# Loading x2 for the last layer's sum into a tile of its own, issued one body earlier

## The chip, the cores and the metric

One core of a Trainium2 chip runs the whole kernel. The metric is device time in microseconds (us), lower is better; where several runs were made the median is given.

## What is computed

The reference is a network of two blocks on an image of 4 x 128 channels x 64 x 64. The first block adds an attention layer and then a recurrence over the 4096 positions. The second adds a stack of eight Mamba layers and then a layer of experts. Around the change it is this line:

```python
x = x + _L1_conv_ref(_ln_c(x), L1_conv_W_in, ...)     # eight Mamba layers, then the sum
```

`_ln_c` normalizes over the channels. Each Mamba layer projects its input, applies a short causal convolution, forms `dA = exp(dt * A)` and `dBx = dt * xc * B` for 16 states a channel, runs `h = dA * h + dBx` along the positions, sums `h * C` over the states, gates the result, projects back and normalizes. The x that the sum takes is the recurrence's output, which the kernel calls x2; the sum is x3.

## The kernel before, in words

The data lies with channels on the 128 partitions and positions along the free axis. The function `mamba` works through 256 bodies: 8 chunks of 512 positions, in each chunk 8 layers, in each layer the 4 images (`bodies`, L1167). Body number i is thus of the last layer where i mod 32 is 28 to 31, and of the first layer of a chunk where it is 0 to 3.

A body is walked through in 16 slots (L1227 to 1256). In each slot, VectorE runs two scans (L1075), the next slot's dBx is made on TensorE (L1042), ScalarE makes dA a few slots ahead (L1020), GpSimd multiplies a group of four states by C in every second slot (L1100), and TensorE adds up products of four slots before (L1104). For the two slots in the middle, 8 and 9 counted from 1, GpSimd makes the scan's input instead of TensorE (L1063).

The rest of the work is put into the slots by hand, in the table `PLAN` (L711), one row for a slot. In a row, what stands left of the bar comes before TensorE adds up, what stands right after it. The letter says whose work it is: o the body whose scans run, n the next one, q the one before, s and z the bodies three and four further on if they are of the first layer. All engines run their instructions in program order, and `manual_schedule` keeps the order as written; so the table is also the order of each queue.

The rows that matter here, numbered from 1:

- row 1, `s.mean` (L838 to 841): the mean of x2 for a body of the next chunk, made in the tile that `z.fetch` filled; row 2 takes its variance
- row 11, `| q.u n.diag q.end`: the norm of the body before (L1154, on VectorE), the load of the next body's diagonal blocks (`diag`, L1014, 1792 KB), and `end` of the body before
- row 12, `n.dtx0` (L979): GpSimd multiplies dt by the input for the next body; `n.turn0` in row 15 turns it on TensorE (L986), and only then can the next body's dBx be made
- row 13, `z.fetch` (L834): loads x2 of a first-layer body four further on, 256 KB
- row 14, `n.C0` (L957): the first of four loads of C for the next body, 1024 KB each

`end` does something only for the last layer's bodies, 32 in all. It takes a tile under the tag "x2", of which there is one buffer, the same that `fetch` and `mean` use; loads x2 into it (L1159); adds the layer's output on GpSimd (L1160); and stores the sum to x3 in DRAM (L1163). All DMAs here are issued by SyncE, which stands at an issue until what that issue must wait for is done; only the last store of all is ScalarE's. The recurrence of the first block runs alongside in the first 220 bodies, some steps in each slot (L670 to 700), with loads and stores of its own on the same queue.

Of the kernel before, what the change touches and what calls it, by code (L numbers as in the profile page):

```python
# [8 lines left out]
F32 = mybir.dt.float32  # L9
# [11 lines left out]
P = 128  # L21
# [19 lines left out]
DEPTH = 8  # L41
# [5 lines left out]
TL = 512  # L47
# [673 lines left out]
n.bt q.ru s.first n.spread n.B n.skip0 |  # L721
| q.u n.diag q.end
n.pt0 n.softplus0 n.pt1 n.dtx0 | o.leave0 n.softplus1
o.back0 | z.fetch
| n.C0
n.turn0 |
n.C1 n.dtx1 | n.skip1 o.gate0
# [19 lines left out]
def mamba(tc, ops, I, rec, x2_d, x3_d):  # L747
# [8 lines left out]
    nc = tc.nc  # L756
# [7 lines left out]
    with ExitStack() as ctx:  # L764
# [8 lines left out]
        w1 = ctx.enter_context(tc.tile_pool(name="mw1", bufs=1))  # L773
# [38 lines left out]
        def bank(what):  # L812

            name = f"f{BANK[what]}"
            return psf.tile([P, TL], F32, tag=name, name=name)
# [27 lines left out]
        def sums(o, of, what):  # L843

            o.ms = bank(what)
            for n in range(NB):
                nc.tensor.matmul(  # L847
                    o.ms[:, n : n + 1], of[:, n * P : (n + 1) * P], ops.avg[:, 0:1],
                    start=n == 0, stop=True, skip_group_check=True,
                )  # L850

        def inverse(o, eps):

            o.r = w.tile([P, NB], F32, tag="r", name="r")
            nc.vector.tensor_scalar(o.r, o.ms[:, 0:NB], eps, None, ALU.add)
            nc.gpsimd.tensor_tensor(o.r, o.r, power, ALU.pow)

        def rows(o, what):

            o.R = bank(what)  # L860
            for n in range(NB):
                nc.tensor.transpose(
                    o.R[:, n * P : (n + 1) * P], o.r[:, n : n + 1].to_broadcast([P, P]), ops.ident
                )
# [287 lines left out]
        def norm(o):  # L1152
            o.out = us[o.b] = up.tile([P, TL], F32, tag="u", name="u")
            nc.vector.tensor_tensor(o.out, o.pos, o.R, ALU.mult)  # L1154

        def end(o):
            here = (slice(None), o.b, slice(o.ck * TL, (o.ck + 1) * TL))
            x3 = w1.tile([P, TL], F32, tag="x2", name="x3")
            nc.sync.dma_start(out=x3, in_=x2_d[here])  # L1159
            nc.gpsimd.tensor_tensor(x3, x3, o.out, ALU.add)  # L1160

            by = nc.scalar if o is bodies[-1] else nc.sync
            by.dma_start(out=x3_d[here], in_=x3)  # L1163
# [5 lines left out]
        def get(i):  # L1169
            return bodies[i] if 0 <= i < len(bodies) else None  # L1170

        def table(name):
            return lambda o: nc.scalar.preload_act_table_set(name)
# [16 lines left out]
            "B": give_b,  # L1190
            "bt": turn_b, "square": square, "pm": lambda o: sums(o, o.sq, "pm"),
            "rstd": lambda o: inverse(o, 1e-5), "ru": lambda o: rows(o, "ru"), "u": norm,
            "end": lambda o: end(o) if o.l == DEPTH - 1 else None, "edge": edge, "edges": add_edge,
            "exp": table(EXP_TANH),
        }
# [21 lines left out]
        for i in range(-2, len(bodies) + 1):  # L1217
            o, n, q = get(i), get(i + 1), get(i - 1)
            who = {"o": o, "n": n, "q": q, "m": get(i + 2), "a": o or q}
            s, z = get(i + 3), get(i + 4)  # L1220
# [362 lines left out]
@with_exitstack  # L1583
def tile_kernel(ctx: ExitStack, tc: tile.TileContext, I, out):
    nc = tc.nc
    const = ctx.enter_context(tc.tile_pool(name="const", bufs=1))
    dram = ctx.enter_context(tc.tile_pool(name="scratch", bufs=1, space=DRAM))
    nc.scalar.preload_act_table_set(EXP_LN)
    ops = Ops(nc, const)
    stats = const.tile([P, B * NBLK, 6], F32, name="stats")  # L1590
    gating_w = gating_weights(tc, const, ops, I)
    x1_d = dram.tile([P, B, L], F32, name="x1_d")
    x2_d = dram.tile([P, B, L], F32, name="x2_d")
    x3_d = dram.tile([P, B, L], F32, name="x3_d")
    wx_d = dram.tile([P, B, L], F32, name="wx_d")

    with tc.manual_schedule():
        with ExitStack() as c:
            conv_layer(tc, ops, I, x1_d, wx_d, stats)
            rec = Recurrence(c, tc, ops, I, stats, wx_d, x1_d, x2_d)  # L1600
            mamba(tc, ops, I, rec, x2_d, x3_d)
        experts(tc, ops, I, gating_w, x3_d, out)
# [90 lines left out]
```

## Time and profile before

| | |
|---|---|
| median of 3 runs | 15102.85 us (15088.36 to 15107.24) |
| the profiled execution, its own time | 15096.43 us |
| its span | 15094.6 us |
| TensorE clock granted in it | 0.978 of full |
| scans of `mamba`, first to last start | 1945.2 to 14807.7 us |
| DMA: moved, mean rate | 1914.56 MB, 127 GB/s |
| diag load, x256 | 1792 KB each, 8.8 us median from issue to landing |
| C load, x1024 | 1024 KB each, 6.7 us median |
| x3 store, x31 on SyncE | 256 KB each, 2.0 us median |

The page of a profile lists busy time by engine (PE is TensorE, PEld its weight loads, DVE is VectorE, ACT is ScalarE, POOL is GpSimd, SPq the DMA queue of SyncE) and groups of equal instructions with busy time, mean duration in ns, and the idle time just before them with what ended it. The timeline lists instructions in order of time: start, duration, engine, line, operation, output and inputs, and in brackets the idle time before it. Tile names have their numbers left out, so x stands for x2 and x3 tiles alike, x_d for the DRAM arrays that hold them. A view of one line of code gives its instructions, what its engine waited for ahead of them, and, for a DMA, the time from issue to landing. A wait for several things is put down to the one that ended last in the profile.

### The profile page before, as it was taken

How to read it: one execution, taken by the hardware profiler on the slowest of the kernel's cores; microseconds unless marked ns; L12 is line 12 of the kernel's file. 1: busy time of each engine (PE TensorE's matmuls, PEld its weight loads, DVE VectorE, ACT ScalarE, POOL GpSimd, SP SyncE). 2: the span in 40 equal slices, each digit the busy share in tenths (PEclk: the TensorE clock that was granted, in tenths of full speed). 3: DMA queues.
4: the chain of work that ended last, by engine and by line, in shares of the span. 5: the costliest groups of instructions: out<-in, count | busy, mean ns of one | idle time of the engine just before them, and what ended most of it. 6: DMA issues, size and time to landing. Idle time of an engine off the chain costs nothing. (4 is left out here: it accounts for less than half of the span.)

```text
span 15094.6 us, 307827 instructions
## 1 busy us (share of the span) xinstructions
PE 14211.8 (94%) x124378; PEld 10858.4 (72%) x124378; DVE 12976.4 (86%) x16043; ACT 10979.7 (73%) x21400; POOL 12587.4 (83%) x5760
## 2 busy tenths in 40 slices
PE   7999989999999999999999999999999999999996
PEld 3444577777777777777777777777777777777774
DVE  8996079998999899989998899989998999889984
ACT  6887267776777677777777777777777777677772
POOL 5664079998999899989998899989998999889983
PEclk8999999999999999999999999999999999999998
DMA  0001034343444343334434333433343344334344
GB/s 23 26 26 35 15 133 145 136 145 136 143 141 141 139 148 139 138 136 149 139 139 147 139 142 136 148 136 139 139 148 137 135 144 148 134 130 146 130 144 180
DMA packets 600045, 1914.56 MB, mean 127 GB/s; under 512 B 347489, under 2 KB 347873, under 8 KB 434273
## 3 DMA queue, kind: packets, MB, share of 16 engines
q1 hardware_dynamic: 598480, 1894.60, 35.6%
q8 instruction: 984, 16.12, 0.4%
q14 instruction: 437, 3.57, 0.1%
q10 hardware_dynamic: 144, 0.26, 0.0%
HBM read 1823.10 MB, written 71.57 MB: 126 GB/s over the span
## 5 line engine op out<-in xcount | busy, mean ns | idle before, releaser
L1100 POOL TENSOR_TENSOR hs<-hs,Cb 128x2048 f32<-128x2048 f32 x2048 | 9295.1, 4540 | 718.5 <-DVE state L1092 547.6
L1075 DVE TENSOR_TENSOR_SCAN hs<-dA,state,dBx 128x512 f32<-128x512 f32 x7168 | 8804.6, 1266 | 919.3 <-PE dBx L1042 772.2
L1020 ACT ACTIVATE dA<-dt,A 128x512 f32<-128x512 f32 x7168 | 4730.3, 716 | 16.3 <-DVE hs L1075 10.2
L1104 PE MATMUL yT<-ident,hs 128*128 128x128 f32 x32768 | 4404.3, 278 | 139.1 <-POOL hs L1100 138.9
L1042 PE MATMUL dBx<-diag,dtxT 64*128 64x128 f32 x57344 | 4214.1, 284 | 24.8 <-DVE hs L1075 18.2
L1104 PEld LDWEIGHTS yT<-ident,hs 128*128 128x128 f32 x32768 | 3803.7, 147 | 548.3 <-issue 354.3
L1042 PEld LDWEIGHTS dBx<-diag,dtxT 64*128 64x128 f32 x57344 | 3526.8, 187 | 803.7 <-issue 746.8
L683 PEld LDWEIGHTS p<-z,vt 128*128 128x128 f32 x8192 | 1283.6, 189 | 854.0 <-ACT z L691 374.2
L691 ACT ACTIVATE z<-p 128x4 f32<-128x4 f32 x4096 | 702.4, 171 | 1514.3 <-PE p L683 1486.6
L683 PE MATMUL p<-z,vt 128*128 128x4 f32 x8192 | 1452.2, 248 | 80.5 <-ACT z L691 71.6
L1075 DVE TENSOR_TENSOR_SCAN hs<-dAp,state,hs 128x512 f32<-128x512 f32 x1024 | 1272.4, 1271 | 296.7 <-POOL hs L1063 296.7
L1063 POOL TENSOR_TENSOR hs<-Bb,dtx 128x512 f32<-128x512 f32 x1024 | 1282.8, 1276 | 0.0
L904 DVE SCALAR_TENSOR_TENSOR xc<-f,taps,xc 128x511 f32<-128x511 f32 (+2 forms) x1536 | 1112.2, 724 | 28.1 <-ACT z L691 24.0
L1020 ACT ACTIVATE dAp<-dt,A 128x512 f32<-128x512 f32 x1024 | 708.8, 692 | 490.6 <-DVE hs L1075 455.8
L279 DVE SCALAR_TENSOR_TENSOR acc<-qp,dww,acc 128x512 f32<-128x512 f32 x1184 | 892.0, 753 | 25.6
L979 POOL TENSOR_TENSOR dtx<-dt,xc 128x512 f32<-128x512 f32 x512 | 651.3, 1272 | 217.5 <-ACT dt L973 217.5
L293 POOL TENSOR_TENSOR off<-off,to 128x512 f32<-128x512 f32 x288 | 366.6, 1273 | 411.3 <-ACT to L291 398.6
L1020 ACT ACT_TABLE_LOAD x511 | 655.6, 1283 | 9.0
L898 ACT ACTIVATE xc<-f,taps 128x512 f32<-128x512 f32 x512 | 350.7, 685 | 426.4 <-PE f L895 293.7
L919 PE MATMUL f<-u,given 128*128 128x512 f32 x1024 | 601.5, 671 | 3.9 <-DVE xc L904 3.8
L847 PEld LDWEIGHTS f<-avg,sq 128*128 128x128 f32 x2048 | 257.4, 197 | 466.2 <-ACT sq L1148 466.2
L895 PE MATMUL f<-u,given 128*128 128x512 f32 x1024 | 567.0, 636 | 0.8 <-DVE u L868 0.8
(235 smaller groups left out, 15145.7 us busy)
## 6 DMA issues: line engine op xcount, KB each, us to landing
Cb<-c_d SPq DMA_DIRECT2D x1024, 1024.0 KB, 6.7
diag<-spare SPq DMA_DIRECT2D x256, 1792.0 KB, 8.8
Bb<-c_d SPq DMA_DIRECT2D x256, 512.0 KB, 4.9
given<-in_m_given_dram SPq DMA_DIRECT2D x64, 640.0 KB, 8.2
slab<-in_w_dram SPq DMA_DIRECT2D x60, 512.0 KB, 9.9
x<-x_d SPq DMA_DIRECT2D x96, 256.0 KB, 3.7
c_d<-dbl SPq DMA_DIRECT2D x512, 32.0 KB, 1.6
x_d<-x SPq DMA_DIRECT2D x63, 256.0 KB, 2.0
```

The costliest lines, as they stand in the source:

```text
L279: nc.vector.scalar_tensor_tensor(rows(to), x, dww[:, t : t + 1], rows(o.acc), ALU.mult, ALU.add)
L683: nc.tensor.matmul(self.p[:, k, :], self.vt, self.before, start=False, stop=True, skip_group_check=True)
L691: nc.scalar.activation(self.z[:, k, :], self.p[:, k, :], AF.Tanh, scale=0.5)
L904: nc.vector.scalar_tensor_tensor(x, o.v[h][:, : TL - k], taps[:, o.l, h, DC - 1 - k : DC - k], x, ALU.mult, ALU.add)
L919: nc.tensor.matmul(o.pz[h], o.given[:, at : at + P], o.u, start=True, stop=True)
L979: nc.gpsimd.tensor_tensor(to, blocks(o.dt[h]), blocks(o.xc[:, h, :]), ALU.mult)
L1020: nc.scalar.activation(o.dA[j][:, k, :], o.dt[h], AF.Exp, scale=A[:, o.l, h, n : n + 1])
L1042: nc.tensor.matmul(o.dBx[j][:, at : at + 64, :], o.dtxT[h][row, n, :], o.diag[row, n, :, 2 * sp : 2 * sp + 2], start=True, stop=True,)
L1063: nc.gpsimd.tensor_tensor(hs[:, k, :].rearrange("p (q n t) -> p q n t", n=NB, q=2), o.Bb[:, k, :].rearrange("p (q n t) -> p q n t", n=NB, ...
L1075: nc.vector.tensor_tensor_scan(hs[:, k, :], o.dA[j][:, k, :], hs[:, k, :] if sp == SP_B else o.dBx[j][:, :, k], state[:, o.l, o.b, h, s : ...
L1100: nc.gpsimd.tensor_tensor(hs, hs, o.Cb[f], ALU.mult)
L1104: nc.tensor.matmul(o.yT[:, n, :], x[:, n * P : (n + 1) * P], ops.ident, start=start and n == 0, stop=True, is_transpose=True, skip_group_c ...
```

## The change

The load in `end` becomes a step of its own, `x3`, that fills a tile under a tag of its own ("x3", again one buffer), and the table puts it into row 13 of the body that it belongs to, ahead of `z.fetch`. `end`, still in row 11 of the body after, takes that tile. Lines are otherwise as before, and 2 KB per partition more of the on-chip memory are used.

```diff
-o.back0 | z.fetch
+o.back0 o.x3 | z.fetch
...
+        def fetch_x(o):
+
+            o.x3 = w1.tile([P, TL], F32, tag="x3", name="x3")
+            nc.sync.dma_start(out=o.x3, in_=x2_d[:, o.b, o.ck * TL : (o.ck + 1) * TL])
+
         def end(o):
             here = (slice(None), o.b, slice(o.ck * TL, (o.ck + 1) * TL))
-            x3 = w1.tile([P, TL], F32, tag="x2", name="x3")
-            nc.sync.dma_start(out=x3, in_=x2_d[here])
+            x3 = o.x3
             nc.gpsimd.tensor_tensor(x3, x3, o.out, ALU.add)
...
+            "x3": lambda o: fetch_x(o) if o.l == DEPTH - 1 else None,
```

## The prediction

> **What bounds the kernel now.** I read the page first. VectorE, GpSimd and TensorE are all close to full, so a stall on one can reach the end, and the scan is what the recurrent stage is paced by:
>
> ```profile
> PE 14211.8 (94%) x124378; PEld 10858.4 (72%) x124378; DVE 12976.4 (86%) x16043; ACT 10979.7 (73%) x21400; POOL 12587.4 (83%) x5760
> ...
> L1075 DVE TENSOR_TENSOR_SCAN hs<-dA,state,dBx 128x512 f32<-128x512 f32 x7168 | 8804.6, 1266 | 919.3 <-PE dBx L1042 772.2
> ```
>
> The scan waits 772.2 us in all for its input dBx from TensorE. To see where, I cut the span at the first scan of each body (32 scans a body, 256 bodies, numbered in their order) and asked for the busy time of the engines by stretch. Columns: stretch, length, busy PE, PEld, DVE, ACT, POOL, clock, DMA.
>
> ```profile
> 3319.20:3368.60 49.40, 48.38 (x448) 38.74 (x447) 45.28 (x52) 37.76 (x73) 46.41 (x21) 1.00 0.46 161
> 3368.60:3427.40 58.80, 52.20 (x459) 42.12 (x458) 46.70 (x56) 39.73 (x76) 47.61 (x21) 0.93 0.40 143
> 3427.40:3487.20 59.80, 52.69 (x459) 42.42 (x459) 46.60 (x54) 38.78 (x74) 47.13 (x21) 0.93 0.37 129
> ```
>
> These are bodies 28, 29 and 30. Body 28 takes 49.4 us, much as those before it; the bodies in which the one before was of the last layer (29, 30, 31, 32 and the same places of each later chunk) take 57.8 to 62.1, with only 1.4 us more VectorE and 1.2 us more GpSimd work. Thirty periods are of this kind: four for each of seven chunks, and two in the last chunk.
>
> The timeline of body 29 shows how the stall arises. VectorE:
>
> ```profile
> 3418.76 0.67 DVE L1136 TENSOR_TENSOR y<-f,gate 128x512 f32<-128x512 f32 x1
> 3427.37 1.28 DVE L1075 TENSOR_TENSOR_SCAN hs<-dA,state,dBx 128x512 f32<-128x512 f32 x1 [7.94 <-PE dBx L1042]
> ```
>
> GpSimd, and below it SyncE's queue:
>
> ```profile
> 3403.83 4.54 POOL L1100 TENSOR_TENSOR hs<-hs,Cb 128x2048 f32<-128x2048 f32 x1 [1.14 <-DVE state L1092]
> 3416.23 1.26 POOL L1160 TENSOR_TENSOR x<-x,u 128x512 f32<-128x512 f32 x1 [7.87 <-DMA x<-x_d]
> 3417.45 1.26 POOL L979 TENSOR_TENSOR dtx<-dt,xc 128x512 f32<-128x512 f32 x1
> ```
>
> ```profile
> 3406.12 0.34 SPq L1014 DMA_DIRECT2D diag<-spare  x1
> 3406.57 0.38 SPq L1159 DMA_DIRECT2D x<-x_d  x1
> 3417.52 0.32 SPq L1163 DMA_DIRECT2D x_d<-x  x1
> 3419.53 0.32 SPq L834 DMA_DIRECT2D x<-x_d  x1
> 3419.90 3.64 SPq L957 DMA_DIRECT2D Cb<-c_d  x2
> ```
>
> The load of x3 (L1159) is issued 0.45 us behind the 1792 KB load of diag. GpSimd is done at 3408.37 and waits 7.87 us for it at the sum (L1160); dtx, next on GpSimd, starts at 3417.45 though its dt was ready near 3409.2 (body 28: dtx at 3358.60, 0.92 us after GpSimd was free). dtx must be turned on TensorE before the next body's dBx can be made, and the first scan of that body is 7.94 us late.
>
> Over all 32 sums, the view of line 1160 lists GpSimd's idle time ahead of it:
>
> ```profile
>   DMA x<-x_d: 93.8, 12
>   DVE state L1092: 74.6, 10
>   DVE hs L1075: 51.1, 6
>   issue: 16.0, 2
>   DVE u L1154: 2.1, 1
> ```
>
> That is 237.6 us. Only 93.8 carry the DMA's name, but the other engines named had been done: in each of the 30 cases the sum begins 8.0 to 10.5 us after the load was issued, and u was ready some 11 us before (3405.45 against 3416.23). The view of line 1159 gives the landing times:
>
> ```profile
> DMA to landing us min/median/max: 2.7/9.1/10.4
> ```
>
> Leaving out the 2.1 us of the very last sum (a true wait for u), 235.5 us, or 7.85 for each of 30, is waiting for this load. VectorE's gaps before the 30 first scans that follow run from 6.9 to 9.5 us and sum to 237.9: the stall goes over to the scan nearly one to one.
>
> **The change, part by part.**
>
> *Load out of slot 11.* Removes GpSimd's 7.85 us wait 30 times. In its place the sum starts at 3408.37, ends at 3409.6, and dtx runs 3409.6 to 3410.9 instead of 3417.45: 7.85 us earlier. The sum's own 1.26 us stays on GpSimd, but 0.92 of it lies where dtx waits for dt anyway, so dtx is 0.4 us later than in body 28. That is covered: the scans of the old body keep VectorE busy to 3419.43. Were the cover gone, it would cost 0.4 x 30 = 12 us. The first scan falls back to 3419.43, a gain of 7.9 us.
>
> A rule of the Trainium skill speaks against so much. "DMA: Bandwidth & Descriptors", section "Anatomy of one DMA — SWDGE (gpsimd) path", gives a DMA about 2.0 us plus its bytes at 436 GB/s: 2.6 us for 256 KB (an estimate, for the GpSimd path). The load would then land at 3409.2 and GpSimd wait 0.8 us: 30 x 0.8 = 24 us to gain. The trace has 2.8 us for the same size when nothing is ahead (x2's load of 3419.53), but a median of 9.1 for this one, behind diag. The row decides: 7.85.
>
> *What is late next.* After the stall, body 29 is 58.80 - 7.94 = 50.9 us, against 49.4: its VectorE does 1.4 us more (mean and first norm of the next chunk). GpSimd's 47.6 us and TensorE's 52.2 stand below or near that; of TensorE's, part is the cold restart (clock 0.93 against 1.00), which goes with the stall. Cold restarts cost something between nothing (body 31: 58.4 - 7.5 = 50.9) and 0.8 us (body 30: 59.8 - 8.1 = 51.7) in the 22 periods that begin so: 0 to 18 us. I take 0.2 each, 4 us, nearer to body 31.
>
> *Load into slot 13 of its own body, with its own tile.* The same number of DMAs, the same bytes, 0.38 us of SyncE's time each. It has a whole body (about 50 us) until its sum, so its landing costs nothing even behind diag (10.4 us at most). The tile has one buffer, so in bodies 29, 30 and 31 of a chunk the load waits until the previous body's x3 is stored. Behind it on SyncE stand the x2 fetch, the Cb loads and, every fourth body, the recurrence's loads. Before, the x2 fetch itself waited for that store (L834 after L1163), so the wait isn't new, only its place.
>
> How long it is, the trace doesn't show: the store will be issued at 3409.7, with diag still in flight. On the near side is its row now, 2.0 us with the queue empty: landing at 3411.7. On the far side is the same page, section "Queues, rings and completion order": each DMA engine takes descriptors in ring order, so the store ends behind diag, where the load ended, at 3406.57 + 9.5 = 3416.1. I take the far end. Then x3's load goes out at 3416.1, x2's at 3416.5, the first Cb at 3416.9. x2 lands 2.8 us later plus 0.8 for 256 KB ahead of it (at the 320 GB/s of the windows where Cb loads run): 3420.1, that is 0.7 us into the next body, whose mean wants it 2.1 us in (L838 at 3370.76, body at 3368.66). Margin 1.4 us, cost nothing. If it is gone, each microsecond costs one in 21 bodies. Cb: median 6.7 us plus 1.6 for the two loads ahead: 3425.2; its product starts 8.4 us into a body (3377.06), at 3427.8. Covered by 2.6 us.
>
> *Sum.* 30 x 7.9 = 237, plus 4 for the clock, is 241, nothing on the other side. The profiled execution's own time is 15096.4 us (span 15094.6); it would become 14855. It lies 6.4 under the median of 15102.85; the median becomes 14862.
>
> **Rivals.**
>
> *A, as worked out:* 14862, own range 14840 to 14890 (7.5 to 8.1 us a stall, clock 0 to 18, the cover of 12 us lost). 84 in 100.
>
> *B, part is given back.* The store lands about 4.4 us later than I take it, so the mean on TensorE, in order ahead of the next dBx, waits 3 us in 21 bodies: 63 us back, 14925. For it: the margin is an estimate of 1.4 us. Against: x2's load behind nothing lands in 2.8 us. 9 in 100.
>
> *C, the change doesn't do what it says:* another wait ends last at the sum (u, or GpSimd's order), and dtx stays where it is: 15103. Against: u was ready 2.9 us before GpSimd was free. 3 in 100.
>
> *D, slower.* SyncE stands at the moved load until the store has landed, and everything behind it, x2 and Cb first, comes late. To eat 241 us and add 30, the mean must wait 271 / 21 = 12.9 us a body, so the store must land 14.3 us after 3416.1, over 20 us after its issue. Nothing of this size on the queue took over 10.5. Its time from there: 15135 and up. 4 in 100.
>
> **How the numbers follow.** Predicted is A, 14862. The range of 14830 to 14910 holds A with its bounds and 10 us for the spread of runs, and reaches part of the way to B. Faster by over 0.2% (30 us, about what a measurement can tell here; the runs before spread over 19) are A and B, 0.93; within it C, 0.03; slower D, 0.04.
>
> **What would show it.** Right: the idle time ahead of the sum falls from 237.6 to under 10 us; the 30 first scans start without a gap; these bodies take about 51 us; the x3 store takes about 6 us to land instead of 2.0; the clock in them is back near 1.00. Wrong: a wait for x2 at L838, a wait for Cb at L1100, or a first scan still waiting for dBx with dtx early.

## The result and the profile after

The changed kernel takes 14893.2 us (median of 4 runs, 14888.06 to 14894.52); the kernel before, with one more run beside it, 15098.8. The ratio is 0.9867, 95% interval 0.9854 to 0.9879: faster by 1.3%, some 206 us, where 241 were forecast. It lies inside the range on record (14830 to 14910), 3 us above the likeliest case's own range, with 31 us to explain.

The stretch view of the changed kernel, cut at the first scans of bodies 29, 30 and 31 (columns as in the prediction: stretch, length, busy PE, PEld, DVE, ACT, POOL, granted clock, DMA share, GB/s):

```profile
3367.48:3418.18 50.70, 49.72 (x460) 40.06 (x459) 46.54 (x55) 38.30 (x74) 47.23 (x21) 1.00 0.35 125
3418.18:3477.28 59.10, 52.50 (x460) 42.58 (x459) 46.57 (x55) 38.67 (x75) 47.30 (x21) 0.94 0.39 136
3477.28:3527.98 50.70, 49.71 (x460) 40.04 (x459) 46.55 (x55) 38.29 (x74) 47.25 (x21) 1.00 0.43 150
```

Bodies 29 and 31 are what was forecast: 50.7 us, with the clock back at 1.00. Body 30 isn't: 59.1 us, at a clock of 0.94, hardly less than its 59.8 before. It is so in each of the first six chunks (57.5 to 61.2 us); in the last two body 30 takes 51.0 and 51.4.

First, the wait that was to go. GpSimd and SyncE in body 29 after the change:

```profile
3402.66 4.53 POOL L1100 TENSOR_TENSOR hs<-hs,Cb 128x2048 f32<-128x2048 f32 x1 [1.14 <-DVE state L1092]
3407.16 1.27 POOL L1164 TENSOR_TENSOR x<-x,u 128x512 f32<-128x512 f32 x1
3408.38 1.27 POOL L979 TENSOR_TENSOR dtx<-dt,xc 128x512 f32<-128x512 f32 x1
```

```profile
3405.21 0.34 SPq L1014 DMA_DIRECT2D diag<-spare  x1
3408.46 0.32 SPq L1167 DMA_DIRECT2D x_d<-x  x1
3415.74 0.32 SPq L1159 DMA_DIRECT2D x<-x_d  x1
3416.11 0.43 SPq L834 DMA_DIRECT2D x<-x_d  x1
3416.59 0.90 SPq L957 DMA_DIRECT2D Cb<-c_d  x2
3417.53 0.57 SPq L664 DMA_DIRECT2D wx<-wx_d  x1
```

The sum follows GpSimd's product without a gap, and dtx follows the sum. Over all 32 sums the view of line 1164 has one wait left, the last one's for u:

```profile
L1164 POOL TENSOR_TENSOR x<-x,u x32: 1260/1272/1298, 3407.2 to 14623.7; 128x512 f32<-128x512 f32 x32
...
  DVE u L1154: 2.1, 1
```

237.6 us of idle time have become 2.1. The 30 first scans begin with no gap, too (between -0.1 and 0.2 us, an overlap of records at the one end).

Second, what came instead. SyncE, having issued the store at 3408.46, stands at the moved load until 3415.74, when the store has landed. This store took 7.3 us to land; the median over all is 6.4, and it was 2.0 before. Then x3, x2, two Cb loads and wx, an input of the recurrence (L664), go out within 2 us of one another. The wx load is scaled on ScalarE by L667, which in the program stands right behind the load. ScalarE in body 30, after the change:

```profile
3428.13 0.60 ACT L667 ACTIVATE wx<-wx,sh,sc 128x256 f32<-128x256 f32 x1 [7.50 <-DMA wx<-wx_d]
```

and VectorE, which needs what ScalarE makes:

```profile
3429.98 0.75 DVE L904 SCALAR_TENSOR_TENSOR xc<-f,taps,xc 128x511 f32<-128x511 f32 x1 [5.50 <-ACT z L691]
...
3436.17 2.45 DVE L1075 TENSOR_TENSOR_SCAN hs<-dA,state,dBx 128x512 f32<-128x512 f32 x2 [2.31 <-PE dBx L1042]
```

wx is issued 0.65 us ahead of body 30's start and lands 10.6 us later, behind everything that had gathered. ScalarE waits 7.5 us, and VectorE loses 5.5 and 2.3. In other bodies that load wx (every fourth, numbers 2 above a multiple of 4) it is issued 3.9 us ahead of the start, and ScalarE waits 0 to 2.1 us. The last two chunks have no such wait, because the recurrence's loads are over by then.

In the kernel before, body 30 had no such wait, in any of the six chunks. In the first, wx left 3.8 us ahead of the body's start and landed 5.1 us later, and ScalarE reached the scaling 2.0 us after that, without waiting for it. SyncE and ScalarE there:

```profile
3423.58 0.57 SPq L664 DMA_DIRECT2D wx<-wx_d  x1
```

```profile
3430.72 0.59 ACT L667 ACTIVATE wx<-wx,sh,sc 128x256 f32<-128x256 f32 x1
```

All waits of line 667 together, the kernel before first and the changed one second:

```profile
  DMA wx<-wx_d: 54.6, 41
```

```profile
  DMA wx<-wx_d: 88.3, 45
```

What body 30 takes beyond 50.7 us sums to 51.4 us over the six chunks. Theory: SyncE's stand at the moved load makes wx late, and ScalarE's wait for it is the price. Rivals: what body 30 has to load is too much wherever SyncE stands; or x2 or C hold it by themselves; or, for the gain itself, it came from the tile of its own and not from the new place.

### The profile page after: what moved, and what is told of

Read it like the earlier page. It is cut to its first block, busy times and chain, and to the rows that moved or that the text cites. A ratio compares the mean times of both kernels' runs of the same rounds, so it can differ in the third digit from the quotient of the medians.

```text
span 14890.3 us, 307789 instructions
## 1 busy us (share of the span) xinstructions
PE 14160.7 (95%) x124378; PEld 10821.2 (73%) x124378; DVE 12974.0 (87%) x16043; ACT 10980.2 (74%) x21400; POOL 12589.8 (85%) x5760
```

## The experiments

Each ran beside the kernel before on one chip. The level differs a little between chips (15082 and 15092 us for the kernel before), so verdicts go by ratio, and a body's time by the profile.

**One part alone: the tile.**

```diff
-            x3 = w1.tile([P, TL], F32, tag="x2", name="x3")
+            x3 = w1.tile([P, TL], F32, tag="x3", name="x3")
```

> One part of the change alone: x3 has a tile of its own, but its load is issued where it was, in row 11 behind the diag load. Theory (the load waits in the queue behind diag, whatever tile it fills): GpSimd waits as before, 7.85 us at 30 sums, and the time stays at 15099, within 15 us. Rival (the shared tile made the load late): the sum starts at once and the time falls to about 14893.

Measured: 15083.6 against 15082.2, ratio 1.0001 (0.9993 to 1.0009). The view of its line 1160 is much as before:

```profile
  DMA x<-x_d: 111.9, 15
  DVE state L1092: 95.0, 13
  issue: 12.6, 2
```

That is 219.5 us of waiting, beside the 2.1 of the very last sum; before it was 235.5. The tile alone gives nothing: the load came as late into a tile of its own.

**The order in the queue alone.** The kernel before (one shared tile, row 11 still), with the load ahead of diag. For this the load is a step of its own, as in the changed kernel; only the table is shown:

```diff
-| q.u n.diag q.end
+| q.u q.x3 n.diag q.end
```

> The kernel before, with one thing changed: in row 11 the x3 load is issued ahead of the diag load instead of behind it (shared tile, same body, same slot). Theory (its 9 us are the 1792 KB ahead of it in the queue): it lands behind Bb alone, near 4 us after its issue; GpSimd waits 1 to 2 us instead of 7.85, and the time falls by 28 x (5.9 to 7.9) less the 51 us of body 30, since x2's fetch in row 13 still stands until the store lands: ratio to before 0.987 to 0.993. Rival (a load at this place takes 9 us whatever is ahead, or diag late by it holds dBx just as long): ratio 0.998 to 1.002.

Measured: 14913.2 against 15092.5, ratio 0.9881 (0.9866 to 0.9896). In its profile the load lands 5.5 us after its issue, by the median, not 9.1, and the waits ahead of the sum are 77.8 us, 2.6 each where I had expected 1 to 2:

```profile
  DMA x<-x_d: 49.3, 19
  DVE hs L1075: 25.3, 10
  issue: 3.2, 1
```

So what was ahead of it in the queue made most of the 7.85 us: changing places with one DMA, with no new slot and no new tile, brings nine tenths of the change's gain. Body 30 pays here as well: it takes 53.1 to 58.7 us, SyncE stands at x2's fetch until the store has landed, and ScalarE waits 3.0 to 4.5 us for wx.

**The load at a place where SyncE needn't stand.** Own tile, but row 4 of the body after:

```diff
-n.v1 | q.leave1 n.tap03
+n.v1 | q.leave1 n.tap03 q.x3
...
-o.back0 o.x3 | z.fetch
+o.back0 | z.fetch
```

> The changed kernel, but the load is issued in row 4 of the following body, where the store before it has long landed and SyncE need not stand. Theory (in the changed kernel SyncE, standing at the load until the store is done, brings the recurrence's wx load late in one body in four; body 30 of six chunks pays 7 to 10 us for it): these bodies fall from 58-61 to about 51 us and the time from 14893 to about 14842. Rival (body 30 is slow for what it has to load at all, not for the stand): it stays near 14893.

Measured: 14844.6 against 15082.2, ratio 0.9840 (0.9827 to 0.9854). Body 30:

```profile
3415.92:3466.66 50.74, 49.76 (x460) 40.05 (x459) 46.58 (x55) 38.91 (x75) 47.27 (x21) 1.00 0.43 152
```

Body 30 is 50.7 us in all six chunks. wx is issued 3.6 us ahead of its start again, and ScalarE waits 0.3 to 1.7 us for it, which costs nothing. The ratio lies close to the changed kernel's (0.9867, 0.9854 to 0.9879), so it is body 30 that decides: the theory is borne out. But this version also takes x3's load out of the burst; the next one separates the two.

**Two buffers for the tile.** Place and bytes as in the changed kernel; only the wait for the store goes:

```diff
-            o.x3 = w1.tile([P, TL], F32, tag="x3", name="x3")
+            o.x3 = w1.tile([P, TL], F32, tag="x3", name="x3", bufs=2)
```

> The changed kernel with two buffers for the x3 tile, so that the load in row 13 doesn't wait for the store before it; its place and bytes are the same. Theory (the stand for the store is what makes wx late): SyncE issues x3, x2 and C at once, wx goes out near 3.9 us ahead of body 30 as in other bodies and waits behind less: at least half of the 51 us comes back, 14843 to 14868, ratio to before 0.983 to 0.985. Rival (the extra 512 KB in the queue, not the stand, make wx late): stays at 14893, ratio 0.987.

Measured: 14841.0 against 15092.5, ratio 0.9832 (0.9819 to 0.9846). SyncE at the end of body 29:

```profile
3408.65 0.32 SPq L1167 DMA_DIRECT2D x_d<-x  x1
3409.02 0.42 SPq L1159 DMA_DIRECT2D x<-x_d  x1
3409.50 0.43 SPq L834 DMA_DIRECT2D x<-x_d  x1
...
3414.75 0.57 SPq L664 DMA_DIRECT2D wx<-wx_d  x1
```

The load goes out 0.37 us behind the store instead of 7.28, wx at 3414.75, 3.6 us ahead of body 30. Body 30 takes 50.7 us in five chunks and 51.4 in one. With the same bytes in the queue nearly all of the 51.4 us is back, so without the stand the traffic costs next to nothing.

**The load in row 4, but in x2's tile.** As the version with row 4, with

```diff
-            o.x3 = w1.tile([P, TL], F32, tag="x3", name="x3")
+            o.x3 = w1.tile([P, TL], F32, tag="x2", name="x3")
```

> The load in row 4 of the following body again, but into the tile under x2's tag, as before the change: no tile of its own. The sum finds its data, but x2's fetch in row 13 must wait for the store as in the kernel before. Theory (a stand of SyncE in row 13 until the store lands, by whichever load, delays wx): body 30 stays at 58 to 61 us and the time at 14893, within 10 us. Rival (it is the moved load's own place): 14842.

Measured: 14862.8 against 15082.2, ratio 0.9854 (0.9841 to 0.9868): neither of the two, but between them. The interval alone reaches both; body 30 decides, with 18.8 us over 50.7 in sum, not 51.4 and not nothing. Its SyncE does stand, at x2's fetch:

```profile
3411.56 0.32 SPq L1167 DMA_DIRECT2D x_d<-x  x1
3418.13 0.32 SPq L834 DMA_DIRECT2D x<-x_d  x1
...
3419.44 0.57 SPq L664 DMA_DIRECT2D wx<-wx_d  x1
```

wx goes out 1.8 us ahead of body 30 in this chunk (0.65 in the changed kernel), and ScalarE waits 4.2 us (7.5); body 30 takes 57.7 us here. Over the chunks waits of 2.1 to 4.3 us go with bodies of 50.9 to 57.7, in the changed kernel waits of 5.9 to 7.5 with 57.5 to 61.2. So a stand of nearly this length, at x2's fetch, costs only part. My expectation took it for all of it. What this version lacks is the moved load at the head of the burst, its issue and its 256 KB; that these make the rest is argued, not shown. Of the 3.3 us between the two waits in the first chunk, 1.2 are the earlier issue and 2.2 the shorter way from issue to landing (8.4 us, not 10.6). By an estimate at the 320 GB/s of the prediction, 256 KB less ahead would make 0.8 of these 2.2; the rest stays open. Why the cost falls faster than the wait is taken up in the last section.

**ScalarE's wait taken away, SyncE as it is.** The changed kernel, the scaling 12 recurrence steps after the load:

```diff
-        nc.scalar.activation(wx, wx, AF.Identity, scale=self.sc, bias=self.sh)
         self.got[n] = wx, x1
+    def scale(self, n):
+        wx = self.got[n][0]
+        self.nc.scalar.activation(wx, wx, AF.Identity, scale=self.sc, bias=self.sh)
...
             self.load(n + 1)
+        if k == RT // 2 + 12 and n + 1 < L // RT:
+            self.scale(n + 1)
```

(the first, ahead of the loop, stays right behind its load).

> The changed kernel, with the scaling of wx on ScalarE (L667) issued 12 recurrence steps after its load instead of right behind it. SyncE's order is untouched. Theory (the wait of ScalarE for wx is what body 30 pays): 51 us off as in the version with row 4, and some 28 us more, since the other bodies that load wx (those with a number 2 above a multiple of 4) run 0.6 us over 48.57 on average, 28.6 us in sum: about 14814. Rival (x2 or C come late too and hold body 30 by themselves): only the 28 us, 14865.

Measured: 14809.9 against 15082.2, ratio 0.9820 (0.9807 to 0.9834). Body 30:

```profile
3414.20:3464.91 50.71, 49.73 (x460) 40.06 (x459) 46.55 (x56) 38.79 (x75) 47.25 (x21) 1.00 0.48 163
```

With SyncE standing as long as ever, body 30 takes 50.7 us in all six chunks: neither x2 nor C was late enough to matter. The other wx bodies fall from 49.17 to 48.57 us on average, 28.6 us in sum.

**The same in the kernel before.**

> The kernel before with the wx scaling 12 steps later and nothing else. Theory (before the change, the 7.9 us stall of the scan in body 30 covered the wait for wx there): it gains only the 33.6 us by which the other wx bodies run over 48.57, ratio 0.9978, against some 83 us that the same edit gives in the changed kernel. Rival (the wait for wx cost body 30 its time before the change too): 80 us, ratio 0.9947.

Measured: 15060.3 against 15092.5, ratio 0.9980 (0.9971 to 0.9989), 32 us. The edit that is worth some 80 us behind the change (by the bodies: 51.4 in body 30 and 28.6 in the others; by the two ratios to before, 71) is worth 32 without it. In its profile the other wx bodies lose 33.4 us in sum; the thirty bodies around the sums take 1772.5 us, as before (1773.9). Body 30 of this kernel:

```profile
3422.54:3481.62 59.08, 52.01 (x459) 41.91 (x458) 46.63 (x55) 38.77 (x74) 47.20 (x21) 0.93 0.39 130
```

So the number is as expected, but my reason for it, that the stall covered a wait for wx, is only half of it. In body 30 of the kernel before ScalarE didn't wait for wx at all. The stall held the sum back, so its store went out at 3417.52, after diag had landed (3415.46), and took 2.0 us; and it put off the body's start, so wx was there in time.

**Both edits.** Row 4 and the late scaling together.

> Both of the edits that helped: the load in row 4 of the following body with its own tile, and wx scaled 12 steps after its load. Theory (wx on ScalarE is the only thing that SyncE's stand made late): no faster than the wx edit alone, ratio 0.982 within 0.0007. Rival (the stand costs something besides, behind C or x2): 0.981 or less.

Measured: 14814.4 against 15092.5, ratio 0.9815 (0.9802 to 0.9829). That is within what was expected of the late scaling alone (0.9820). The interval also reaches the rival's 0.981, so the bodies decide: its 30 bodies sum to 1525.2 us against 1528.0. Whatever else the stand costs is no more than these 3 us. Either of the two versions with the late scaling beats both kernels, by 1.8% and about 0.5%.

## Why the prediction was right, and where it was short

- *The load's wait goes, 30 times 7.9 us: right.* Gaps before the 30 first scans summed to 237.9 us and now to -2.2: 240 us against 237. That the row (9.1 us to land) was to be taken and not the 2.6 us from the Trainium skill ("DMA: Bandwidth & Descriptors", section "Anatomy of one DMA — SWDGE (gpsimd) path") is settled by the version with the two DMAs exchanged, where it takes 5.5 us with less ahead, and by the changed kernel, where it takes 2.8 by the median.
- *What is late next, 50.9 us a body: right* for 24 of the 30, which take 49.6 to 51.8 us (mostly 50.7 in bodies 29 and 31, and 51.5 in body 32).
- *The cold restart, 4 us: within its bounds.* The 30 bodies fell from 1773.9 to 1577.0 us; with body 30's 51.4 set apart that is 248.3, so 8 us beyond the stalls, within the 0 to 18 given. Nothing here separates the clock's part in these 8 from the rest.
- *The store behind diag, landing 6 us after its issue, and SyncE standing so long: right.* 6.4 us by the median; in body 29 diag lands at 3415.10, the store at 3415.72, and the load goes out at 3415.74 where I had put 3416.1. That descriptors are taken in ring order, from which I reasoned, doesn't by itself say in which order they end; the trace does, for this place.
- *The cost of that stand, nothing: wrong, and this is the step that failed.* I named what is queued behind the moved load, "x2 fetch, the Cb loads and, every fourth body, the recurrence's loads", and then worked out a margin for the first two only. Those two margins held. The third had none: its consumer on ScalarE follows the load at once, and in other bodies of the kernel before it waited already, up to 3.0 us. I read "so the wait isn't new, only its place" as harmless; but the old stand was 2.0 us long and lay behind the stall, while the new one is about 6.4, and what has gathered behind it goes out in one burst. The version with two buffers (no stand) and the one with the late scaling (no wait on ScalarE) each bring body 30 back to 50.7 us. The term is 51.4 us where I had 0.
- *The rest of the kernel, nothing:* it gained 7.4 us between the two profiled executions, 5.0 of it in the other wx bodies (33.6 over 48.57 before, 28.6 after), whose waits vary from body to body; the tile-only version has 25.9 there, so this is no effect of the change. Sum: 240.1 + 8.2 - 51.4 + 7.4 = 204.3, the difference of the spans. Against my 241, the missing 51.4 us were made up by 14.7 from terms that ran the other way, half of it no effect of the change, and the range reached 20 us past A's own on the side of B. That the number fell within it is in part luck.
- *The rivals.* The outcome is B's in its size of loss (51 us back, 63 forecast), but not in its mechanism: the waits for x2 at L838 are what they were (11.4 us in both kernels), and no 21 bodies pay 3 us; six pay 8.6. D named the path, SyncE standing and what is behind it late, but put x2 and C there, and a size that didn't come. C didn't come.

## What to carry to other kernels

When a DMA's wait is moved on a queue, list every DMA behind it up to the next one that would have waited anyway, and work out a margin for the consumer of each, above all for one that stands right behind its load in an engine's program order. When a long stall goes, the loads of its stretch lose the time that it gave them, those too that show no wait. Here wx left 3.8 us ahead of a start that was to come 7.9 us sooner, with no wait on record, and an edit worth 32 us before was worth some 80 after. So count each load's margin from the new start before the gain is booked; a list of waits isn't enough. And of a load that waits long, ask first what is ahead of it in its queue: here, an exchange of two issues gave nine tenths of the gain.

## What was not expected of the hardware

ScalarE's wait for wx isn't paid at its length. In body 30 of the versions in which only wx can be late, bodies whose granted TensorE clock stayed at 1.00 take 50.7 us and what the wait has beyond some 1.9 us: 50.7 with waits of 0.3 to 1.8 us, 51.4 with 2.6 (two buffers), 52.0 with 3.1 (row 4, x2's tile). Where the clock was halved for a while they take more: 57.5 to 61.2 us with waits of 5.9 to 7.5 in the changed kernel, at mean clocks of 0.89 to 0.94. By an estimate from these figures (39.4 us of waits, less six times 1.9), 28 of the 51.4 us are the waits themselves, and the other 23 go with the halved clock. It is also part of why the version with the load in row 4 and x2's tile paid so little: its waits were shorter, and three of its six bodies kept the full clock. In the body shown, TensorE had been idle for 5.6 us, and its clock was 0.50 from 3430 to 3434, when it came back.

The other wx bodies show the same on a small scale. These two of the changed kernel waited 1.38 and 1.39 us (columns as above):

```profile
4410.27:4459.26 48.99, 47.55 (x446) 38.34 (x445) 45.22 (x52) 38.07 (x74) 45.10 (x19) 1.00 0.42 143
5209.32:5259.89 50.57, 49.12 (x446) 39.31 (x445) 45.33 (x53) 38.07 (x74) 45.07 (x19) 0.97 0.40 141
```

The second holds one stretch of 3.4 us at half clock, some 25 us into the body, though TensorE had been busy for 2.5 of the 3.4 us ahead of it, and is 1.6 us longer. What brings that stretch isn't known: a wait of 1.13 us went with one, and a wait of 2.10 us with none. No run changed the clock alone, so its share is read off the traces and not shown by experiment.
